# Layer 0 of an attention kernel: queries turned by VectorE in 32x32 blocks, output weights over 32 rows by head, four token quarters abreast

## The chip, the cores and the metric

The kernel runs on one core of one Trainium2 chip. A core has TensorE (PE in the profile; PEld is its weight loads), VectorE (DVE), ScalarE (ACT), GpSimd (POOL), and SyncE (SP), which here issues every DMA. The metric is the device time of one execution in microseconds; lower is better.

## The reference

Two layers, each a residual block over x of shape (16, 64, 64, 256) in f32. The change lies in layer 0, linear attention over the 4096 tokens of an image, with 8 heads of 32:

```
x = x + L0(gn(x))                       # gn: group norm, 32 groups
q, k, v = split(gn(x) @ w_qkv)          # 256 -> 3 * 256, each as 8 heads of 32
q = softmax(q over the 32 of a head) * 32**-0.5
k = softmax(k over the 4096 tokens)
context[h] = k[h] @ v[h].T              # 32 x 32 for a head
out = context[h].T @ q[h]; L0 = out @ w_out
x = x + L1(gn(x))                       # local attention, 7x7 windows, not changed
```

## The kernel before

Images run one after the other, 16 in all. An image is held as two tiles of 128 channels by 4096 tokens (`img`), `x` raw and `xn` normalised. Tokens are in 8 strips of 512; `strip(s)` is a strip's slice and `ORDER` the order in which layer 0 takes the strips. PE, ACT, DVE and SP run in the order in which the program is written (`manual_schedule`); an instruction that waits holds what is behind it on its engine. PSUM is used as two double banks, `double` (pd in the profile, handed out in turn by `psum2` and `bank`), and four single banks, `single` (ps).

Layer 0 of an image (`layer0`) goes through 16 pieces of 256 tokens:

- `queries_keys(p)`: PE multiplies tokens by the query and key weights (L514), ACT takes the exponential (L518), DVE sums the 32 of a head (L521) and takes the reciprocal (L523), POOL multiplies the query part by it (L524). The result `e` holds 128 tokens by 256 query and 256 key columns, twice.
- `context(p - 1)`: PE adds keys by tokens into `pc`, two banks of `single` (L532). The value weights come later, so the moving operand is the raw tokens `xtok`, loaded by DMA into one of two window buffers (`window`).
- `transposed(p - 2)`: four PE transposes (L546) of 128x128 turn the queries, so that the features of four heads lie on the 128 partitions; DVE (L552, even pieces) or ACT (L550, odd ones) copies them to `qq`.

Every second piece DVE also normalises the next strip (L283, through `normalise`).

After the 16 pieces, DVE scales and centres the context (L572, L573), and `output_weights` folds it with the value and output weights to `w2`, 256 by 256: transposes of the context (L301), a scaling (L306), products with the value weights (L311), the block diagonal of the heads (L319), products with `w_out` (L322), a scaling to `w2` (L323). For every strip PE then multiplies `qq` by `w2` (L587: for each half of the channels two matmuls of 128x128 by 512 columns that accumulate), DVE adds the result to x (L596) and takes the statistics for the next group norm (L473).

Then come the group norm of layer 1 (`group_steps`, L260 to L279), positional products (L630, evacuated to `qq` by DVE and ACT in turn, L621 and L619), values (L678), keys and queries (L704), and local attention for two groups of heads (L766 scores, L774 exponential, L784 and L797 weighted sums, `finish` with the block transposes L810 and L817). During local attention the next image is loaded and its first strips are normalised; the outputs of strips 1, 2 and 0 are stored last. `positional_products` takes its pairs of strips from `ORDER`; the values, keys and queries have an order of their own, `KEYED`.

Of the kernel before, what the change touches and what calls it, by code (L numbers as in the profile page):

```python
# [14 lines left out]
ALU = mybir.AluOpType  # L15
# [4 lines left out]
P = 128  # L20
W = 64
C = 256
HEADS, HD = 8, 32
NS = 8
# [9 lines left out]
SCALE = HD**-0.5  # L34
# [5 lines left out]

UNITS = (1, 2, 3, 0)
KEYED = (2, 3, 4, 5, 6, 7, 1, 0)
ORDER = (3, 4, 5, 6, 7, 1, 2, 0)
EDGE = (5, 3)


# [309 lines left out]
def attention_fast(tc, io, ok):  # L356


    nc = tc.nc
    with ExitStack() as ctx:  # L360
# [3 lines left out]
        double = [ps.tile([P, 2, 512], F32, tag=f"pd{i}", name=f"pd{i}") for i in range(2)]  # L364
        single = [ps.tile([P, 512], F32, tag=f"ps{i}", name=f"ps{i}") for i in range(4)]
        turn = [0, 0]

        def psum2():
            turn[0] += 1
            return double[turn[0] % 2]  # L370

        def banks():

            i = turn[1] % 4
            turn[1] += 1
            if i >= 2:
                return single[2 * i - 4 : 2 * i - 2], (0, 1)
            return [double[i][:, j] for j in range(2)], (i, i)
# [8 lines left out]
        n = Net(tc, cp, io)  # L387
# [3 lines left out]
        with tc.tile_pool(name="zeros", bufs=1) as zp:  # L391
# [3 lines left out]
            for v in vpad:  # L395
                rows = v.rearrange("a r w c -> a r (w c)")
# [7 lines left out]
            for d in pos:  # L404
                for i in range(2):
                    part = d[:, RING + 8 * i : RING + 8 * i + 8].rearrange("a s h w -> a (s h w)")
# [5 lines left out]
        qq = cp.tile([P, 2, NT], F32, tag="qq", name="qq")  # L412
# [7 lines left out]
        w2 = cp.tile([P, 2, C], F32, tag="w2", name="w2")  # L420
# [23 lines left out]
        def work_tile(name):  # L444
            return work.tile([P, 1024], F32, tag="work", name=name)

        def window(name):
            return vwin.tile([P, 2 * NB * P], F32, tag="vw", name=name)

        def watch(total, x, w):  # L450
            nc.gpsimd.tensor_tensor(total[:, :w], total[:, :w], x, ALU.add)  # L451

        def strip(s):
            return slice(s * 512, (s + 1) * 512)

        def halves(b):

            return [img[0][0], img[1][b % 2]], [img[0][1], img[1][1 - b % 2]]

        def load_half(b, k):  # L460
            x = halves(b)[0][k]
            for s in ORDER:
                nc.sync.dma_start(x[:, strip(s)], xc[b, :, k, strip(s)])
# [8 lines left out]
        def strip_stats(st, x, k, s):  # L472
            nc.vector.bn_stats(st[:, k, s], x[k][:, strip(s)])  # L473

        def stats_tile(name):
            return small.tile([P, 2, NS, 6], F32, tag="st", name=name)
# [23 lines left out]
        def layer0(b, x, xn, mean, rstd, xtok, ready):  # L500

            mu = None
            pc, other = single[:2], single[2:]
            eq = {}

            def first(p):
                return ORDER[p // 2] * 512 + (p % 2) * 2 * P

            def queries_keys(p):
                ps = psum2()  # L510
                for t in range(2):
                    n0 = first(p) + t * P
                    for k in range(2):
                        nc.tensor.matmul(  # L514
                            ps[:, t], xn[k][:, n0 : n0 + P], n.wqkv_sb[:, k, : 2 * C], start=(k == 0), stop=(k == 1)
                        )
                e = work_tile(f"eq{b}_{p}").rearrange("p (t c) -> p t c", t=2)
                nc.scalar.activation(e, ps, AF.Exp)  # L518
                q4 = e[:, :, :C].rearrange("p t (h d) -> p t h d", d=HD)
                z = small.tile([P, 2, HEADS], F32, tag="qz", name=f"qz{b}_{p}")  # L520
                nc.vector.tensor_reduce(z, q4, AX.X, ALU.add)  # L521
                r = small.tile([P, 2, HEADS], F32, tag="qr", name=f"qr{b}_{p}")
                nc.vector.reciprocal(r, z)  # L523
                nc.gpsimd.tensor_tensor(q4, q4, r.unsqueeze(3).to_broadcast([P, 2, HEADS, HD]), ALU.mult)  # L524
                watch(tops, r.rearrange("p t h -> p (t h)"), 2 * HEADS)
                watch(others, z.rearrange("p t h -> p (t h)"), 2 * HEADS)
                return e

            def context(p):
                for t in range(2):  # L530
                    for hg in range(2):
                        nc.tensor.matmul(  # L532
                            pc[hg][:, : C + 1],
                            eq[p][:, t, C + hg * P : C + (hg + 1) * P],
                            xtok[p // 4][:, 2 * (p % 4) + t],
                            start=(p == 0 and t == 0),
                            stop=(p == 15 and t == 1),
                        )

            def transposed(p):  # L540
                pt = other[p % 2]
                e = eq.pop(p)
                for hg in range(2):
                    for t in range(2):
                        i = 2 * hg + t
                        nc.tensor.transpose(pt[:, i * P : (i + 1) * P], e[:, t, hg * P : (hg + 1) * P], n.ident)  # L546
                dst = qq[:, :, first(p) : first(p) + 2 * P]
                src = pt.rearrange("p (g c) -> p g c", g=2)
                if p % 2:
                    nc.scalar.copy(dst, src)  # L550
                else:
                    nc.vector.tensor_copy(dst, src)  # L552

            for p in range(16 + 1):
                if p < 16:
                    if p % 2 == 0 and p // 2 + 1 < NS and p // 2 + 1 >= ready:
                        normalise(xn, x, mean, rstd, ORDER[p // 2 + 1])
                    eq[p] = queries_keys(p)
                if p == 1:
                    mu = n.spread(mean, lambda name: other[1], small, f"{b}")  # L560
                if 1 <= p <= 16:
                    context(p - 1)
                    if p % 4 == 0 and p // 4 + 1 < 4:
                        xtok[p // 4 + 1] = load_tokens(b, p // 4 + 1)
                if p >= 2:
                    transposed(p - 2)

            r = small.tile([P, 2, 1], F32, tag="krz", name=f"krz{b}")
            z = small.tile([P, 2, 1], F32, tag="kz", name=f"kz{b}")
            cc = work_tile(f"cc{b}")[:, : 2 * C].rearrange("p (a c) -> p a c", c=C)  # L570
            for hg in range(2):
                nc.vector.reciprocal(r[:, hg], pc[hg][:, C : C + 1])  # L572
                nc.vector.scalar_tensor_tensor(cc[:, hg], pc[hg][:, :C], r[:, hg], mu, ALU.mult, ALU.subtract)  # L573
            transposed(15)
            cT = work_tile(f"cT{b}")[:, :512].rearrange("p (a c) -> p a c", c=P)
            n.output_weights(cc, rstd, bank, cT, w2, f"{b}")
            for hg in range(2):
                nc.vector.tensor_copy(z[:, hg], pc[hg][:, C : C + 1])
            watch(tops, r.rearrange("p a b -> p (a b)"), 2)
            watch(others, z.rearrange("p a b -> p (a b)"), 2)  # L580

            st = stats_tile(f"st1_{b}")
            for s in ORDER:
                py, _ = banks()
                for hg in range(2):
                    for co in range(2):
                        nc.tensor.matmul(  # L587
                            py[co],
                            w2[:, hg, co * P : (co + 1) * P],
                            qq[:, hg, strip(s)],  # L590
                            start=(hg == 0),
                            stop=(hg == 1),
                        )
                for co in range(2):
                    xv = x[co][:, strip(s)]
                    nc.vector.tensor_tensor(xv, py[co], xv, ALU.add)  # L596
                for k in range(2):
                    strip_stats(st, x, k, s)
            return st

        def scale(to, w, rstd):
# [258 lines left out]
        with tc.manual_schedule(engines=ORDERED):  # L860
            x, xn = halves(0)
            st = stats_tile("st0_0")
            for k in range(2):
                load_half(0, k)
            for k in range(2):
                for s in ORDER:
                    strip_stats(st, x, k, s)
            gn = n.group_stats(st, 1e-5, small, bank, "0_0")
            xtok = {q: load_tokens(0, q) for q in range(2)}
            for s in ORDER[:2]:  # L870
                normalise(xn, x, *gn, s)
            for b in range(B):
                more = b + 1 < B
                x, xn = halves(b)
                st = layer0(b, x, xn, *gn, xtok, 2)
                mean, rstd = n.group_stats(st, 1e-5, small, bank, f"1_{b}")
                scale(wpos, n.wpos, rstd)
# [27 lines left out]
                if more:  # L905
                    st = stats_tile(f"st0_{b + 1}")
# [434 lines left out]
```

## Time and profile before

| | |
|---|---|
| time, median of 3 runs | 6052.62 us (6047.84 to 6058.84) |
| the profiled execution, its own time | 6068.61 us |
| its span in the trace | 6066.8 us |
| mean granted TensorE clock | 0.962 |
| PE busy | 5506.4 us (91%), 76913 matmul records |
| DVE, ACT, POOL busy | 2874.6 us (47%), 2254.7 us (37%), 1029.9 us (17%) |
| from one image's first L514 to the next's | 367.6 to 378.9 us |
| of that, to the start of L587 | 95.2 to 98.2 us |

Durations in the prediction are from the profiled execution, mostly from the second image (first L514 at 468.2 us), and its own time is 2 us longer than its span. A row of a group gives engine, operation, the tile that is written and those that are read, the shape (for PE the array's rows by columns used, then the shape of the moving operand), the count, then busy time and mean duration. An f32 matmul stands as two records, one for each pass, except a transpose, which is one. Durations of PE records have the latency in them; the distance between starts is what they cost in a stream. The chain that ended last is followed back from the last instruction; its list in order of time shows for each piece the start, the length, and the engine, tile and line, with the number of records.

### The profile page before, as it was taken

The page shows a single profiled execution, that of the slowest core. Times are in us where ns is not written, and L with a number is a line of the kernel's source. Part 1 is how long each engine was busy: PE and PEld are TensorE (multiplying, and loading weights), DVE is VectorE, ACT ScalarE, POOL GpSimd, SP SyncE. Part 2 cuts the span into 40 slices and gives each one's busy share as a digit, 9 for nine tenths or more (in the row PEclk, how much of TensorE's full clock was granted, in tenths as well). Part 3 has the DMA queues.
Part 4 walks back from the last instruction along what each step waited for, and adds up shares of the span by engine and source line. Part 5 has one row for each costly group of instructions (what it writes and reads, how often), then busy time and mean ns, then how long its engine had stood idle before and what let it go on. Part 6 is the DMA issues. An engine that isn't in the chain of part 4 may idle for free.

```text
span 6066.8 us, 171741 instructions
## 1 busy us (share of the span) xinstructions
PE 5506.4 (91%) x76913; PEld 3771.3 (62%) x76913; DVE 2874.6 (47%) x5034; ACT 2254.7 (37%) x3233; POOL 1029.9 (17%) x1945
## 2 busy tenths in 40 slices
PE   3999999898999989999898999999989999898998
PEld 2575665656656566665666657566565665756666
DVE  2544545445354444455444554454544545445354
ACT  0252433515334152342524425143252433415334
POOL 2012120211202113021120201212022120111202
PEclk9999999999999999999999999999999999999999
DMA  4341723516244252443515435163350724417234
GB/s 112 76 104 37 133 80 79 115 45 129 59 96 104 48 121 59 102 104 66 110 44 114 99 74 103 37 129 84 73 112 31 144 66 83 104 39 141 59 76 82
DMA packets 737035, 526.94 MB, mean 87 GB/s; under 512 B 240400, under 2 KB 667664, under 8 KB 733712
## 3 DMA queue, kind: packets, MB, share of 16 engines
q1 hardware_dynamic: 736288, 515.86, 38.9%
q8 instruction: 605, 9.91, 0.7%
q14 instruction: 142, 1.16, 0.1%
HBM read 357.02 MB, written 158.73 MB: 85 GB/s over the span
## 4 chain that ended last, share of the span: by engine, by line
PE 88%; ACT 4%; issue 4%; DVE 2%; SPq 1%; DMA 0%; POOL 0%; ACTq 0%; DVEq 0%; POOLq 0%
PE pd L766 16%; PE ps L797 16%; PE pd L514 15%; PE pd L704 7%; PE ps L532 7%; PE ps L704 5%; ACT qq L619 4%; PE pd L587 4%; PE ps L678 4%; PE pd L678 4%; PE ps L587 4%; PE ps L630 2%; PE ps L546 2%; PE ps L784 1%; SPq L399 1%
## 5 line engine op out<-in xcount | busy, mean ns | idle before, releaser
L774 ACT ACTIVATE e<-pd 128x896 f32<-128x896 f32 (+2 forms) x1152 | 928.5, 839 | 1132.0 <-PE pd L766 1129.4
L766 PE MATMUL pd<-qq,kaug 64*64 64x140 f32 (+5 forms) x27648 | 1052.3, 294 | 218.4 <-ACT e L774 143.5
L766 PEld LDWEIGHTS pd<-qq,kaug 64*64 64x64 f32 x27648 | 923.8, 140 | 354.4 <-issue 163.6
L514 PE MATMUL pd<-wqkv,img 128*128 128x512 f32 x2048 | 923.3, 595 | 1.7 <-DVE img L283 1.6
L797 PE MATMUL ps<-e,vw 128*32 128x112 f32 (+1 forms) x18432 | 853.8, 260 | 63.4 <-issue 63.0
L797 PE MATMUL ps<-e,ones 128*32 128x112 f32 (+1 forms) x18432 | 846.5, 256 | 59.7 <-issue 59.2
L810 DVE STREAM_TRANSPOSE r<-ps 128x512 f32<-128x512 f32 x256 | 168.8, 696 | 1437.6 <-PE ps L797 1437.3
L451 POOL TENSOR_TENSOR others<-others,rc 128x16 f32<-128x16 f32 x256 | 113.1, 442 | 2981.5 <-DVE rc L815 2981.5
L518 ACT ACTIVATE eq<-pd 128x1024 f32<-128x1024 f32 x256 | 261.9, 1023 | 943.3 <-PE pd L514 943.3
L514 PEld LDWEIGHTS pd<-wqkv,img 128*128 128x128 f32 x2048 | 372.6, 191 | 380.6 <-issue 353.3
L797 PEld LDWEIGHTS ps<-e,vw 128*32 128x32 f32 x18432 | 502.9, 113 | 154.9 <-issue 117.7
L797 PEld LDWEIGHTS ps<-e,ones 128*32 128x32 f32 x18432 | 546.5, 114 | 72.4 <-issue 71.8
L619 ACT ACTIVATE qq<-ps,bias 32x512 f32<-32x512 f32 (+2 forms) x544 | 320.2, 622 | 718.1 <-PE ps L630 712.5
L521 DVE TENSOR_REDUCE qz<-eq 128x16 f32<-128x512 f32 x256 | 175.5, 685 | 830.5 <-ACT eq L518 830.5
L532 PE MATMUL ps<-xtok,eq 128*128 128x257 f32 x2048 | 486.1, 380 | 0.0
L532 PEld LDWEIGHTS ps<-xtok,eq 128*128 128x128 f32 x2048 | 386.1, 190 | 149.0 <-issue 107.1
L830 POOL TENSOR_TENSOR img<-img,r 128x320 f32<-128x320 f32 (+1 forms) x512 | 421.5, 844 | 164.8 <-DVE rc L815 163.5
L619 ACT ACTIVATE kaug<-pd,bias 32x512 f32<-32x512 f32 x256 | 173.7, 679 | 633.6 <-PE pd L704 630.7
L473 DVE BATCH_NORM_STATS2 st<-img 128x6 f32<-128x512 f32 x512 | 319.9, 677 | 66.1 <-DMA img<-in_xc 66.1
L621 DVE TENSOR_SCALAR qq<-ps,bias 32x512 f32<-32x512 f32 x384 | 309.3, 806 | 6.8
L524 POOL TENSOR_TENSOR eq<-eq,qr 128x512 f32<-128x512 f32 x256 | 274.7, 1073 | 30.7 <-DVE qr L523 1.2
L821 DVE TENSOR_TENSOR r<-r 128x512 f32<-128x512 f32 x256 | 222.3, 868 | 27.5 <-DVE r L817 0.5
(126 smaller groups left out, 6170.0 us busy)
## 6 DMA issues: line engine op xcount, KB each, us to landing
vw<-vpad SPq DMA_DIRECT2D x512, 288.0 KB
img<-in_xc SPq DMA_DIRECT2D x256, 256.0 KB
xtok<-in_xt SPq DMA_DIRECT2D x64, 1024.0 KB
out<-img SPq DMA_DIRECT2D x256, 256.0 KB
vpad<-v SPq DMA_DIRECT2D x112, 512.0 KB
qq<-pos SPq DMA_DIRECT2D x128, 256.0 KB
qq<-in_ring SPq DMA_DIRECT2D x128, 256.0 KB
pos<-qq SPq DMA_DIRECT2D x128, 112.0 KB
```

What stands on the lines that cost most here:

```text
L473: nc.vector.bn_stats(st[:, k, s], x[k][:, strip(s)])
L514: nc.tensor.matmul(ps[:, t], xn[k][:, n0 : n0 + P], n.wqkv_sb[:, k, : 2 * C], start=(k == 0), stop=(k == 1))
L532: nc.tensor.matmul(pc[hg][:, : C + 1], eq[p][:, t, C + hg * P : C + (hg + 1) * P], xtok[p // 4][:, 2 * (p % 4) + t], start=(p == 0 and t = ...
L587: nc.tensor.matmul(py[co], w2[:, hg, co * P : (co + 1) * P], qq[:, hg, strip(s)], start=(hg == 0), stop=(hg == 1),)
L619: nc.scalar.activation(dst, src, AF.Identity, bias=bias)
L621: nc.vector.tensor_scalar(dst, src, bias, None, ALU.add)
L678: nc.tensor.matmul(pi[:, t], x[k][:, n0 : n0 + P], wv[:, k], start=(k == 0), stop=(k == 1))
L704: nc.tensor.matmul(ps[a], wgt[:, k, hg * P : (hg + 1) * P], x[k][:, strip(pair[a])], start=(k == 0), stop=(k == 1),)
L766: nc.tensor.matmul(to, kaug[pl][rows, u, 8 * c : 8 * c + 8].rearrange("p r w -> p (r w)"), q, start=True, stop=True,)
L774: nc.scalar.activation(e, ps[:, :, : 2 * m], AF.Exp)
L797: nc.tensor.matmul(dst, ones if to is zs[j] else vw[:, j, c, h * HD : (h + 1) * HD], pr, start=False, stop=(c == NB - 1),)
L830: nc.gpsimd.tensor_tensor(yv, xv, by_rows(add[:, :, a - w0 : e - w0], xv), ALU.add)
```

## The change

The queries are turned by DVE instead of PE. A DVE transpose of 128x256 turns each 32x32 block by itself, so a quarter of 32 tokens stays on its 32 partitions, which then hold the 32 features of a head; the heads lie one after the other in the free dimension. `qq` is seen as `qv`: partitions (quarter, feature), then 8 heads by 1024 tokens. The output weights are thus needed per head over 32 rows, once in each of the four row groups: `w4`, which takes one of the window buffers. It is made by products of 32 columns whose moving operand repeats a head's context four times, and products over 32 rows. The output product then runs one matmul of 32 rows by 128 columns by 256 tokens for each head, quarter and channel half; the four quarters go to four banks. Results are added per quarter, with a stride in x. `ORDER` is now made of pairs of neighbouring strips, since the product takes 1024 tokens at a time; the host packs the tokens in the same order.

```diff
--- before.py
+++ after.py
@@ -40,7 +40,7 @@
 
 UNITS = (1, 2, 3, 0)
 KEYED = (2, 3, 4, 5, 6, 7, 1, 0)
-ORDER = (3, 4, 5, 6, 7, 1, 2, 0)
+ORDER = (4, 5, 6, 7, 0, 1, 2, 3)
 EDGE = (5, 3)
 
 
@@ -503,6 +503,8 @@
             pc, other = single[:2], single[2:]
             eq = {}
 
+            qv = qq.rearrange("p g (h n) -> p (g h) n", h=4)
             def first(p):
                 return ORDER[p // 2] * 512 + (p % 2) * 2 * P
 
@@ -537,19 +539,12 @@
                             stop=(p == 15 and t == 1),
                         )
 
-            def transposed(p):
-                pt = other[p % 2]
+            def turned(p):
                 e = eq.pop(p)
-                for hg in range(2):
-                    for t in range(2):
-                        i = 2 * hg + t
-                        nc.tensor.transpose(pt[:, i * P : (i + 1) * P], e[:, t, hg * P : (hg + 1) * P], n.ident)
-                dst = qq[:, :, first(p) : first(p) + 2 * P]
-                src = pt.rearrange("p (g c) -> p g c", g=2)
-                if p % 2:
-                    nc.scalar.copy(dst, src)
-                else:
-                    nc.vector.tensor_copy(dst, src)
+                for t in range(2):
+                    T = 2 * p + t
+                    nc.vector.transpose(qv[:, :, HD * T : HD * T + HD], e[:, t, :C].rearrange("p (h d) -> p h d", d=HD))
 
             for p in range(16 + 1):
                 if p < 16:
@@ -563,7 +558,7 @@
                     if p % 4 == 0 and p // 4 + 1 < 4:
                         xtok[p // 4 + 1] = load_tokens(b, p // 4 + 1)
                 if p >= 2:
-                    transposed(p - 2)
+                    turned(p - 2)
 
             r = small.tile([P, 2, 1], F32, tag="krz", name=f"krz{b}")
             z = small.tile([P, 2, 1], F32, tag="kz", name=f"kz{b}")
@@ -571,31 +566,77 @@
             for hg in range(2):
                 nc.vector.reciprocal(r[:, hg], pc[hg][:, C : C + 1])
                 nc.vector.scalar_tensor_tensor(cc[:, hg], pc[hg][:, :C], r[:, hg], mu, ALU.mult, ALU.subtract)
-            transposed(15)
-            cT = work_tile(f"cT{b}")[:, :512].rearrange("p (a c) -> p a c", c=P)
-            n.output_weights(cc, rstd, bank, cT, w2, f"{b}")
+            turned(15)
+            ct = work_tile(f"ct{b}")
+            cT, ch = ct[:, :512].rearrange("p (a c) -> p a c", c=P), ct[:, 512:768]
+            for hg in range(2):
+                for k in range(2):
+                    nc.tensor.transpose(
+                        other[0][:, (2 * k + hg) * P : (2 * k + hg + 1) * P], cc[:, hg, k * P : (k + 1) * P], n.ident
+                    )
+            for k in range(2):
+                dst = cT[:, 2 * k : 2 * k + 2].rearrange("p a b -> p (a b)")
+                nc.vector.tensor_scalar(dst, other[0][:, k * C : (k + 1) * C], rstd[:, k : k + 1], None, ALU.mult)
+            for hg in range(2):
+                for k in range(2):
+                    for h in range(4):
+                        rows = slice(HD * h, HD * h + HD)
+                        nc.tensor.matmul(
+                            other[1][rows, hg * P : (hg + 1) * P].rearrange("p (a d) -> p a d", a=4),
+                            n.wqkv_sb[:, k, 2 * C + hg * P + HD * h : 2 * C + hg * P + HD * h + HD],
+                            cT[:, 2 * k + hg, rows].unsqueeze(1).to_broadcast([P, 4, HD]),
+                            start=(k == 0),
+                            stop=(k == 1),
+                        )
+            nc.vector.tensor_scalar(ch, other[1][:, :C], SCALE, None, ALU.mult)
+            for hg in range(2):
+                for h in range(4):
+                    rows = slice(HD * h, HD * h + HD)
+                    nc.tensor.matmul(
+                        double[h // 2][:, h % 2, hg * C : (hg + 1) * C],
+                        ch[rows, hg * P : (hg + 1) * P],
+                        n.wout_sb[rows, hg],
+                        start=True,
+                        stop=True,
+                    )
             for hg in range(2):
                 nc.vector.tensor_copy(z[:, hg], pc[hg][:, C : C + 1])
+            w4 = window(f"w4_{b}")[:, : 8 * C].rearrange("p (h g c) -> p h g c", h=4, g=2)
+            for h in range(2):
+                nc.vector.tensor_copy(w4[:, h].rearrange("p g c -> p (g c)"), double[0][:, h])
+            nc.scalar.copy(w4[:, 2:4].rearrange("p h g c -> p h (g c)"), double[1])
             watch(tops, r.rearrange("p a b -> p (a b)"), 2)
             watch(others, z.rearrange("p a b -> p (a b)"), 2)
 
             st = stats_tile(f"st1_{b}")
-            for s in ORDER:
-                py, _ = banks()
-                for hg in range(2):
-                    for co in range(2):
-                        nc.tensor.matmul(
-                            py[co],
-                            w2[:, hg, co * P : (co + 1) * P],
-                            qq[:, hg, strip(s)],
-                            start=(hg == 0),
-                            stop=(hg == 1),
-                        )
+            for i in range(NS // 2):
+                s0 = ORDER[2 * i]
                 for co in range(2):
-                    xv = x[co][:, strip(s)]
-                    nc.vector.tensor_tensor(xv, py[co], xv, ALU.add)
-                for k in range(2):
-                    strip_stats(st, x, k, s)
+                    py = [double[a // 2][:, a % 2, : 2 * P] if co else single[a][:, : 2 * P] for a in range(4)]
+                    for h in range(4):
+                        for hg in range(2):
+                            for a in range(4):
+                                rows = slice(HD * a, HD * a + HD)
+                                nc.tensor.matmul(
+                                    py[a],
+                                    w4[rows, h, hg, co * P : (co + 1) * P],
+                                    qv[rows, 4 * hg + h, 8 * HD * i : 8 * HD * (i + 1)],
+                                    start=(h == 0 and hg == 0),
+                                    stop=(h == 3 and hg == 1),
+                                )
+                    xv = x[co][:, s0 * 512 : (s0 + 2) * 512].rearrange("p (t a n) -> p a t n", a=4, n=HD)
+                    if co:
+                        for a in (0, 2):
+                            part = double[a // 2][:, :, : 2 * P].rearrange("p a (t n) -> p a t n", n=HD)
+                            nc.vector.tensor_tensor(xv[:, a : a + 2], part, xv[:, a : a + 2], ALU.add)
+                    else:
+                        for a in range(4):
+                            nc.vector.tensor_tensor(xv[:, a], py[a].rearrange("p (t n) -> p t n", n=HD), xv[:, a], ALU.add)
+                    for s in (s0, s0 + 1):
+                        strip_stats(st, x, co, s)
             return st
 
         def scale(to, w, rstd):
```

## The prediction

> **What bounds the kernel now.** I read the page first: engine totals, then the chain that ended last.
>
> ```profile
> PE 5506.4 (91%) x76913; PEld 3771.3 (62%) x76913; DVE 2874.6 (47%) x5034; ACT 2254.7 (37%) x3233; POOL 1029.9 (17%) x1945
> ...
> PE 88%; ACT 4%; issue 4%; DVE 2%; SPq 1%; DMA 0%; POOL 0%; ACTq 0%; DVEq 0%; POOLq 0%
> ...
> PE pd L766 16%; PE ps L797 16%; PE pd L514 15%; PE pd L704 7%; PE ps L532 7%; PE ps L704 5%; ACT qq L619 4%; PE pd L587 4%; PE ps L678 4%; PE pd L678 4%; PE ps L587 4%; PE ps L630 2%; PE ps L546 2%; PE ps L784 1%; SPq L399 1%
> ```
>
> TensorE is busy 91% and holds 88% of the chain, so what leaves TensorE's stream shortens the time. The change touches L546 (query transposes, 2%) and L587 (output product, 4% + 4%). The chain in order of time, over layer 0 of the second image, shows the stage (start, length, work):
>
> ```profile
> 544.49 3.44 PE pd L514 x8
> 547.92 1.74 PE ps L532 x8
> 549.66 0.44 PE ps L546 x4
> 550.09 3.44 PE pd L514 x8
> ...
> 557.44 0.45 PE ps L546 x4
> 557.89 0.03 issue
> 557.91 0.69 DVE qq L552
> 558.61 0.08 DVE krz L572
> ...
> 563.34 7.13 PE pd L587 x16
> ...
> 584.21 6.88 PE ps L587 x16
> 591.09 0.02 issue
> 591.12 0.69 DVE img L596
> 591.81 1.19 DVE st L473 x2
> ```
>
> A piece of 256 tokens is 3.44 + 1.74 + 0.44 = 5.6 us of TensorE without a gap; nothing else is in the chain there. From the end of L514 (553.53) to the start of L587 (563.34) come 9.8 us of short dependent steps, the "turn". L587 is again TensorE alone; 6.87 us for 16 records of 512 columns is 0.429 us each, 0.839 ns per column and pass (an f32 matmul is two records). After L587 statistics follow, and TensorE waits until 596.88.
>
> **What tells how four row groups behave.** No f32 product of the kernel before uses 32 rows; three things come near. The timeline of TensorE shows L784, which has the very tile shape (32 rows by 128 columns, four row groups, four banks), in bf16:
>
> ```profile
> 320.42 0.39 PE L784 MATMUL ps<-zb 32*128 32x512 bf16 x4
> 320.74 0.32 PE L797 MATMUL ps<-e,vw 128*32 128x64 f32 x8
> ```
>
> The next work starts 0.32 us after the first of the four. One after another at the f32 pass's 0.429 us they would need 1.7 us, and at half of that 0.86. The chain gives the f32 tiles of layer 1:
>
> ```profile
> 679.90 1.68 PE pd L766 x37
> 681.58 1.67 PE ps L797 x64
> ```
>
> Each row covers two window steps. A step of L766 has 12 matmuls in 64x64 tiles (two row halves, two column halves), of 14 x 10, 14 x 16 and 14 x 6 columns: 3584 column passes, which alone would take 3.0 us; two steps in 1.68 us means 3.6 abreast, of four. L797 (four column groups of 32, 16 matmuls of 112 columns a step) gives 3.6 too.
>
> **The Trainium skill.** "TensorEngine Tiling (Array Packing)", Tiling Modes and Gotcha 1: row tiles of 32 rows run independently if they write different banks. The change gives each quarter its own bank; L784 agrees. "TensorE: Matmul & The Clock Gate", Part 3, Measured speedup: four row tiles of K=32, N=512 gave 3.07x; the 3.6 above is better, since it is a stream. Same page, LDWEIGHTS: a load costs its columns, whatever the rows. The trace agrees in order: 190 ns for 128 columns (L587), 140 for 64 (L766), 113 for 32 (L797). Same page, Part 1: idle of about 3.4 us halves the clock. The trace agrees: granted clock 0.75 in 591 to 597 and 0.79 in 597 to 606.
>
> **The change, part by part, per image.**
>
> Transposes of the pieces. The 64 of L546 go. Thirteen groups of four stand ahead of the last L514: 13 x 0.44 = **5.7 us off**. The other three lie in the turn. With them go 8 VectorE copies of 0.69 us (L552) and 8 ScalarE copies of 0.59 (L550), both hidden. Added are 32 VectorE block transposes of 128x256. L810 takes 0.696 us for 128x512, and an operation from PSUM costs 0.69 at 512 elements (L596) and 0.424 at 256 (L323), so 256 elements are worth 0.27: estimate 0.44 us each, 0.35 apart when queued. VectorE per piece: reduction 0.69, reciprocal 0.25, transposes 0.8, half of two normalisations 0.87, together 2.6 of 5.2 us, hidden behind TensorE. Queued behind them are the next normalisation and reduction; ScalarE and POOL then have the same slack as before. Bounds: 0.35 to 0.9 us each (the destination is eight runs 4 KB apart); even 0.9 leaves the piece hidden (3.6 of 5.2), but the turn grows.
>
> The turn. L514 ends at 553.53, the two last L532 groups at 557.0. VectorE is free of the reciprocal at 555.79, then has four transposes, until 557.3. The reciprocal of the key sums starts there, not at 558.52; the two centred contexts take 1.27 as now: 558.6. The last two transposes stand ahead of the scaling of the turned context: 559.4 (now 560.32). From there to the last product of L311 takes 1.87 now; sixteen 32-column matmuls, four abreast, stream the same 8 x 0.107: 561.3. One scaling of 128x256, 0.42: 561.7. Eight 32-row products, two rounds of two passes of 0.215, and about 0.27 of load and latency: 562.8. The first copy of weights, 0.69: the output product starts at about 563.6 against 563.34: **0.3 us on** (bounds: 0.5 off to 2 on). VectorE's second copy is there by 564.2, wanted at 564.5; ScalarE copies the other half in 1.02 us (L518's 1024 elements), wanted at 565.3.
>
> Output product. 32 matmuls of 512 columns become 256 of 256: 128 rounds of four passes, 128 x 256 x 0.839 ns = 27.5 us, the same as 64 x 0.429. L797's round costs 0.104 against 0.094 of streaming; 128 such margins are 1.3 us. Bounds 0 to 1.3; I take half, **0.7 us on**, since longer streams hide more. VectorE's evacuation per 1024 tokens: four adds of 0.42, two of 0.69, four statistics of 0.68, together 5.8 of 6.9 us: hidden.
>
> End of it. Both column halves used to end one after the other; now all four banks of the last half end together, and two adds and two statistics follow: 0.6 + 0.69 + 1.19 = 2.5 us against 1.9: **0.6 us on**.
>
> Clock. The turn has more idle on TensorE and the wait after it is longer. In 8 of the 16 images the trace has the half clock in the turn, and the output product starts 96 us after the first L514 instead of 95.2; I allow that in the other half too: **0.5 us on** (bounds 0 to 2).
>
> Order of strips. Loads, stores, tokens and normalisation follow it. What comes earlier is strip 0: normalised ahead of piece 8, not 14. Its buffer's store is the last of attention, issued on SP's queue by 476.6, and the DMA share is 0 from 480; the normalisation comes after the fifth piece's reduction, near 498. Hidden by 18 us; without that cover VectorE would hold the next reduction. In the ring positions strip 0's edge pieces move from ScalarE to VectorE, about 0.5 us, behind TensorE's L630 and L889. The copied weights take one of two window buffers; the load that reuses it is queued after all value stores, past 635. No new wait on SP or POOL.
>
> Sum: -5.7 + 0.3 + 0.7 + 0.6 + 0.5 = -3.6 us an image, -58 us for 16. The profiled execution took 6068.6 us (span 6066.8): 6011. The median of three is 16 us (0.26%) below it: **5995 us**.
>
> **Rivals.**
> 1. Weight loads stick out (ends slower). 256 columns of streaming hide less than 512. If each round waited for its load, 128 x 0.107 us (L546 shows one 128-column load and one 128-column pass per 0.109 us) = 13.7 us an image: 16 x 10.1 = +162, 6215 us. It decides from 28 ns exposed per round, where 3.6 us is used up. For it: loads of 128 columns are twice L766's. Against: L766 runs a load and a pass every 35 ns, so loads of different tiles overlap each other and the streaming.
> 2. Row groups share something in f32. Two abreast: +27.5 - 3.6 an image, 6434 us; none: +82.5 - 3.6, 7257 us. Against: L784 and L766, whose two row halves write the same partitions.
> 3. The gain is eaten in the gaps: transposes at 0.9 us add 1.8 to the turn, or the slow clock comes each time (2 us): 6020 to 6055 us. For it: the turn already hangs on VectorE. That the change does not do what it says would be this: VectorE's turning would show up in the chain in place of L546.
>
> **How the numbers follow.** Forecast 0.68, within 5950 to 6030; rival 3 0.15; rival 1 0.10; rival 2 0.07. About 0.2% (12 us) is what a measurement can tell from no change. Faster: 0.68 and most of rival 3, 0.78; same 0.04; slower 0.18. The range, 5950 to 6060, leaves out rivals 1 and 2.
>
> **What would show it.** Right: pieces 5.17 us apart in the chain, no L546; the output product 27.5 to 29 us of TensorE an image, with some 0.22 us per round; block transposes of 128x256 at 0.4 to 0.5 us outside the chain. Wrong: an output product above 31 us (rivals 1, 2), or VectorE entries between L514 groups (rival 3).

## The result and the profile after

The changed kernel takes 6006.96 us (median of 5 runs, 6002.63 to 6025.9) against 6052.62: a ratio of 0.9927 with a 95% interval of 0.9909 to 0.9946. It is faster by 0.7%; the forecast was 5995. Its profiled execution took 6006.96 us, with a span of 6005.2 us against 6066.8.

The page of the changed kernel, engine totals:

```profile
PE 5397.6 (90%) x83633; PEld 3876.1 (65%) x83633; DVE 2954.2 (49%) x5562; ACT 2196.0 (37%) x3089; POOL 1025.1 (17%) x1945
```

TensorE has 6720 more matmul records and 109 us less of busy time; VectorE has 80 us more. The chain on this page follows only 2% of the span back, so it can't stand beside the chain of before. I use timelines of one engine, and for each image the distances between the first records of the same lines. Four groups of the changed kernel follow: L547 stands in place of L546, L550 and L552, L637 (with L634) in place of L596, L623 in place of L587 (other lines moved: L514 is L516, L630 is L671, L678 is L719):

```profile
L547 DVE STREAM_TRANSPOSE qq<-eq 128x256 f32<-128x256 f32 x512 | 181.1, 394 | 0.3 <-issue 0.2
L637 DVE TENSOR_TENSOR img<-ps,img 128x256 f32<-128x256 f32 x256 | 90.7, 417 | 103.6 <-PE ps L623 103.6
L623 PE MATMUL ps<-qq,w 32*128 32x256 f32 x4096 | 246.4, 390 | 12.4 <-DVE w L608 12.4
L623 PE MATMUL pd<-qq,w 32*128 32x256 f32 x4096 | 232.2, 374 | 0.0
```

The block transposes cost 0.394 us each, and VectorE sat idle ahead of them for only 0.3 us in the whole execution: what they read was there when VectorE came to them. The two L623 groups hold TensorE for 246 + 232 = 479 us; before, the two L587 groups held it for 229 + 225 = 454.

From the third on, the pieces stand 5.17 us apart, as forecast. This is TensorE's timeline of the changed kernel at the end of layer 0 of the fifth image:

```profile
1689.98 3.63 PE L623 MATMUL ps<-qq,w 32*128 32x256 f32 x64
1693.44 3.63 PE L623 MATMUL pd<-qq,w 32*128 32x256 f32 x64
1700.47 0.59 PE L266 MATMUL pd<-gn,grp 128*128 128x2 f32 x2 [3.40 <-DVE gn L263]
1701.89 0.59 PE L275 MATMUL pd<-gnd,grp 128*128 128x2 f32 x2 [0.84 <-DVE gnd L272]
1703.81 3.68 PE L671 MATMUL ps<-img,wposn 128*64 128x512 f32 x8 [1.32 <-DVE wposn L644]
1707.27 0.59 PE L653 MATMUL pd<-gnm,wposn 128*64 128x1 f32 x8
1707.66 6.39 PE L671 MATMUL ps<-img,wposn 128*64 128x512 f32 x24
1713.99 1.13 PE L930 MATMUL pd<-wvn,gnm 128*128 128x256 f32 x4
1716.78 0.48 PE L719 MATMUL pd<-wvn,img 128*128 128x256 f32 x1 [1.66 <-DVE bvn L933]
```

A half product is 64 records of 256 columns, and the next starts 3.46 us later: 16 rounds of four at 0.216 us, against 0.215 of pure streaming (256 x 0.839 ns). The four quarters run fully abreast, and the loads of weights are hidden. The last row was not foreseen: the first value product waits 1.66 us for VectorE's bias sum (L933). In the sixth image the same place has no wait:

```profile
2080.26 1.13 PE L930 MATMUL pd<-wvn,gnm 128*128 128x256 f32 x4
2081.22 7.07 PE L719 MATMUL pd<-wvn,img 128*128 128x256 f32 x32
```

From the answer on that line of the changed kernel, TensorE's matmuls alone:

```profile
L719 PE MATMUL pd<-wvn,img x1024: 379/379/483, 235.7 to 5783.7; 128*128 128x256 f32 x171
...
  DVE bvn L933: 14.7, 8
```

The second of these rows stands under the times that the engine sat idle ahead of the line: 14.7 us in 8 times, 1.8 us each. They fall in every second image, the first, third, fifth and so on. For the kernel before (L678) no idle time stands there.

Where each image's time stands, in us between starts of records, mean of the 16 images. The sum is the distance from image to image, mean of the 15 full ones, and the row above it is what is left of that sum:

| step | before | after | forecast of the difference | measured |
|---|---|---|---|---|
| first to last L514 record (pieces) | 85.03 | 79.29 | -5.7 | -5.74 |
| to the first output product (turn) | 10.83 | 10.62 | +0.3 | -0.21 |
| to the last output record | 27.28 | 28.32 | +0.7, clock +0.5 | +1.04 |
| to the aggregation L260 | 2.43 | 2.94 | +0.6 | +0.51 |
| to the first positional product | 3.97 | 3.94 | 0 | -0.03 |
| to the first value product | 10.26 | 11.71 | 0 | **+1.45** |
| to the next image | 232.29 | 231.89 | 0 | -0.40 |
| sum | 372.09 | 368.71 | -3.6 | -3.38 |

The step to the first value product takes 12.92 us in the images with the wait and 10.49 in the others. The step to the next image varies by some 10 us from image to image in both kernels (228 to 238 us), so its -0.40 can't be told from nothing.

### The profile page after: what moved, and what is told of

The parts are those of the page before. It is cut to its first block, busy times and chain, and to the rows that moved or that the text cites. A ratio compares the mean times of both kernels' runs of the same rounds, so it can differ in the third digit from the quotient of the medians.

```text
span 6005.2 us, 185440 instructions
## 1 busy us (share of the span) xinstructions
PE 5397.6 (90%) x83633; PEld 3876.1 (65%) x83633; DVE 2954.2 (49%) x5562; ACT 2196.0 (37%) x3089; POOL 1025.1 (17%) x1945
## 5 line engine op out<-in xcount | busy, mean ns | idle before, releaser
L807 PE MATMUL pd<-qq,kaug 64*64 64x224 f32 (+5 forms) x27648 | 1043.4, 293 | 237.3 <-ACT e L815 144.8
L516 PE MATMUL pd<-wqkv,img 128*128 128x512 f32 x2048 | 922.4, 594 | 1.6 <-DVE img L283 1.6
L516 PEld LDWEIGHTS pd<-wqkv,img 128*128 128x128 f32 x2048 | 388.6, 190 | 392.2 <-issue 358.4
L520 ACT ACTIVATE eq<-pd 128x1024 f32<-128x1024 f32 x256 | 262.2, 1024 | 1013.3 <-PE pd L516 1010.6
L662 DVE TENSOR_SCALAR qq<-ps,bias 32x512 f32<-32x512 f32 (+2 forms) x416 | 313.1, 761 | 7.0
L623 PE MATMUL ps<-qq,w 32*128 32x256 f32 x4096 | 246.4, 390 | 12.4 <-DVE w L608 12.4
```

The source lines that it names most:

```text
L516: nc.tensor.matmul(ps[:, t], xn[k][:, n0 : n0 + P], n.wqkv_sb[:, k, : 2 * C], start=(k == 0), stop=(k == 1))
L623: nc.tensor.matmul(py[a], w4[rows, h, hg, co * P : (co + 1) * P], qv[rows, 4 * hg + h, 8 * HD * i : 8 * HD * (i + 1)], start=(h == 0 and h ...
L662: nc.vector.tensor_scalar(dst, src, bias, None, ALU.add)
L807: nc.tensor.matmul(to, kaug[pl][rows, u, 8 * c : 8 * c + 8].rearrange("p r w -> p (r w)"), q, start=True, stop=True,)
```

## The experiments

Each run's ratio is to the kernel before, run beside it on the same chip: 6053.73 us for the first four, 6062.35 for the next four, 6059.93 for the last.

**The wait at the values.** `psum2` and `bank` hand out the two double banks in turn. The old layer 0 took 21 of them (16 pieces, 5 in `output_weights`), the new one takes 16. The rest of an image takes 77 (2 in the statistics, 3 with the biases, 72 in the scores), so that an image took 98 turns, an even number, and now takes 93, an odd one. The value products start in double bank 0 always (`banks` has a counter of its own). The bias product L930 used to fall into the other bank in every image; now its bank alternates, and in every second image it falls into that same bank. One more turn makes the count even again:

```diff
                         strip_stats(st, x, co, s)
+            psum2()
             return st
```

> The changed kernel with one more turn of the double banks at the end of layer 0, so that the bias product for the values (L930 in the changed kernel) again falls into the other bank than the first value products (L719). Theory A (the miss against the forecast is a bank collision: the change asks for 16 double banks in layer 0 instead of 21, so the first value product waits for VectorE's bias sum behind 7.8 us of positional evacuations): the step from the first positional product to the first value product falls from 11.7 us (mean of the 16 images) to some 10.2, 1.5 us an image, 24 us in all, about 5983 us (ratio to the kernel before 0.988 to 0.989). Rival B (that wait is taken up later, or the step is long because the half clock falls there): the step or what follows stays long and the time is within 6 us of 6007.

Measured: 5990.04 us, 0.9875 (0.985 to 0.9899). The step to the first value product is 10.63 us, and no image has the wait. VectorE's queue is as long as before, but TensorE no longer waits for it; these are TensorE's and VectorE's timelines of e1_other_bank around the same place:

```profile
1701.79 1.13 PE L931 MATMUL pd<-wvn,gnm 128*128 128x256 f32 x4
1702.75 5.56 PE L720 MATMUL pd<-wvn,img 128*128 128x256 f32 x25
```

```profile
1696.90 7.66 DVE L663 TENSOR_SCALAR qq<-ps,bias 32x512 f32<-32x512 f32 x10
1704.59 0.42 DVE L934 TENSOR_TENSOR bvn<-bv,pd 128x256 f32<-128x256 f32 x1
```

The values start at 1702.75, ahead of the bias sum at 1704.59. Theory A stands as to the collision, though it put the wait in every image: of the 24 us that it asked for, 17 came back by the medians and by the steps, 31 by the ratios to the kernel before, whose intervals are wide. The step ends where the changed kernel's images without the wait stand (10.49), not at the 10.26 of before; what else lies in it is the half clock, further below.

The same line put into the kernel before, at the end of its `layer0`:

> The kernel before with the same one turn of the double banks at the end of layer 0, nothing else. Theory A: the same collision arises without the change: VectorE ends its evacuations and the bias sum at 1719.3 us in the fifth image where TensorE wants the bank at 1716.9, so up to 2.4 us an image, 24 to 38 us slower than before (6077 to 6090 us). Rival B: the collision needs strip 0 among VectorE's evacuations or the changed pairs: within 0.2% of before.

Measured: 6076.71 us, 1.0035 (1.0023 to 1.0047). The step goes from 10.26 to 11.22 us in the mean: 12.53 in every second image and 9.90 in the others. The wait appears in the kernel before, where the line is L679 (TensorE's matmuls alone):

```profile
L679 PE MATMUL pd<-wvn,img x1024: 379/379/634, 240.2 to 5859.2; 128*128 128x256 f32 x171
...
  DVE bvn L893: 18.0, 8
```

18.0 us of waiting in 8 images go with 21 us of time (23 by the medians). That is just under theory A's span of 24 to 38 us, which had the wait in all 16 images; 8 times its 2.4 us would be 19. The collision needs nothing of the change but an odd count of turns.

**The transposes.** Put back on TensorE for pieces 0 to 12, read by nobody:

```diff
                 e = eq.pop(p)
+                for i in range(4 if p < 13 else 0):
+                    nc.tensor.transpose(
+                        other[p % 2][:, i * P : (i + 1) * P], e[:, i % 2, (i // 2) * P : (i // 2 + 1) * P], n.ident
+                    )
                 for t in range(2):
```

> The changed kernel with the TensorE transposes of pieces 0 to 12 put back, their results read by nobody; VectorE still turns the queries. Theory A (the gain is the 13 x 0.44 us that left TensorE's stream ahead of the last L514): 5.7 us an image, 91 us, about 6098 us, pieces 5.6 us apart. Rival B (the gain came from the copies taken off ScalarE and VectorE, or the pieces are bound elsewhere): within 20 us of 6007.

Measured: 6093.59 us, 1.0055 (1.0033 to 1.0077). That is 87 us above the changed kernel by the medians and 77 by the ratios, where 91 were expected. The last L516 stands again at 84.97 us after the first. The gain in the pieces is what left TensorE's stream: VectorE turned the queries here too, with ScalarE and VectorE free of the copies.

**The order of strips**, alone in the kernel before:

```diff
-ORDER = (3, 4, 5, 6, 7, 1, 2, 0)
+ORDER = (4, 5, 6, 7, 0, 1, 2, 3)
```

> The kernel before with the new order of strips alone (4 5 6 7 0 1 2 3). Theory A (the order is hidden, 18 us between the store of strip 0 and its normalisation): within 0.2% of before. Rival B (strip 0's pieces on VectorE or its late store cost something): 0.5 us or more an image, 8 us or more slower, seen between positional products and values or as a wait of the normalisation.

Measured: 6058.91 us, 1.0004 (0.9991 to 1.0016). No step moves by more than 0.2 us. The order is hidden, as theory A has it.

**The four quarters abreast.**

```diff
-                    for h in range(4):
-                        for hg in range(2):
-                            for a in range(4):
+                    for a in range(4):
+                        for h in range(4):
+                            for hg in range(2):
```

> The changed kernel with the output product's loop over the four quarters outermost: eight matmuls of one row group in a row, then the next quarter's. Same instructions, same count. Theory A (four row groups stream at the same time, and only if they stand next to each other in the stream): the groups come one after another, 256 matmuls x 2 passes x 0.216 us = 110 us an image instead of 27.5, 82 us an image, about 7320 us. Rival B (the engine reorders across row groups by itself, or the product is bound by something else than the streams): far less, within 300 us of 6007.

Measured: one run of 8262.28 us. The output product lasts 168.7 us an image. Theory A holds as to the cause, and its size is off twice. The windows of the first image's product tell why (columns: length, then busy time and count of each engine, then the granted clock):

```profile
190.00:350.00 160.00, 160.00 (x485) 131.33 (x484) 20.63 (x37) 0.00 (x0) 0.00 (x0) 0.50 0.00 0
```

TensorE is never idle by its records, yet the clock is at one half throughout. In the first 2 us, at full clock, a pass starts every 0.216 us; then every 0.427 within a quarter. 512 x 0.427 would be 219 us; at the seams between quarters passes of both overlap, and 169 are left. At full clock that would be some 84 us, an estimate by halving, against 27.5 abreast.

**The half clock in the turn.** In 7 images of the changed kernel the half clock comes within the turn, and in 6 of them it reaches into the output product. Fillers (matmuls whose result nobody reads) in e1_other_bank, ahead of the context's transposes, of the value products and of the 32-row products, and after these:

```diff
+            def filler(bank, k):
+                for _ in range(k):
+                    nc.tensor.matmul(bank, zb, zb[:, :1].to_broadcast([P, 512]), start=True, stop=True)
             ct = work_tile(f"ct{b}")
+            filler(double[1][:, 0], 4)
...
+            filler(double[1][:, 0], 2)
...
+            filler(other[0], 2)
...
+            filler(other[0], 3)
```

> e1_other_bank with 11 bf16 matmuls of 512 columns in the idle gaps of the turn (4 ahead of the context's transposes, 2 ahead of the value products, 2 ahead of and 3 after the 32-row products), into banks that nobody reads. Theory A (the half clock in the turn costs the difference between disturbed and undisturbed images, last output product at 117.98 us in the mean against 116.77): no half clock in the turn, 1.2 us an image, 19 us below e1_other_bank (5990): about 5971. Rival B (zeros do not count as activity for the clock, or the fillers delay the short steps by as much): within 6 us of e1_other_bank, with the half clock still in the turn or the product's start later than 89.23.

Measured: 5969.92 us, 0.9849 (0.9827 to 0.9871). The second image's turn and the first 8 us of its output product, first e1_other_bank, then e6_warm_turn (the granted clock is the third figure from the end):

```profile
546.00:558.00 12.00, 9.24 (x75) 5.94 (x73) 6.18 (x19) 1.84 (x2) 1.84 (x5) 0.81 0.01 1
558.00:566.00 8.00, 8.00 (x96) 6.82 (x100) 1.90 (x6) 0.19 (x1) 0.00 (x0) 0.64 0.01 2
```

```profile
541.00:551.00 10.00, 9.44 (x79) 5.68 (x79) 6.04 (x19) 1.70 (x2) 1.84 (x5) 1.00 0.01 3
551.00:559.00 8.00, 7.99 (x148) 7.60 (x152) 4.03 (x9) 0.33 (x1) 0.00 (x0) 1.00 0.01 2
```

0.81 and 0.64 become 1.00, in every image, and the last output record stands at 116.91 us after the first L516 in the mean, not 117.98. The two ratios' intervals just overlap; the trace's 1.1 us an image are 17 us. Theory A holds by the trace.

**VectorE's queue in the turn.**

```diff
-                if p >= 2:
+                if 2 <= p < 16:
                     turned(p - 2)
...
-            turned(15)
...
                 nc.vector.tensor_scalar(dst, other[0][:, k * C : (k + 1) * C], rstd[:, k : k + 1], None, ALU.mult)
+            turned(14)
...
             watch(others, z.rearrange("p a b -> p (a b)"), 2)
+            turned(15)
```

> e1_other_bank with VectorE's transposes of piece 14 moved behind the scaling of the turned context, and those of piece 15 behind the copies of the weights, so that neither stands ahead of the context's steps. Theory A (VectorE's queue is what the turn hangs on): the output product starts 0.4 to 0.5 us earlier (88.8 instead of 89.23 after the first L516), 7 us in all. Rival B (the chain of the turn is TensorE's and the waits' alone): start unchanged at 89.2, no difference.

Measured: 5987.69 us, 0.9879 (0.9859 to 0.99): by the times not told apart from e1_other_bank. By the trace the output product starts 88.87 us after the first L516 in every image but the first (theory A: 88.8), and VectorE now waits for the last context product, where in the changed kernel it came late to it. VectorE's timelines, first of the changed kernel (the four transposes, then straight on), then of e7_late_turn:

```profile
1661.81 1.36 DVE L547 STREAM_TRANSPOSE qq<-eq 128x256 f32<-128x256 f32 x4
1663.09 0.13 DVE L567 RECIPROCAL krz<-ps 128x1 f32<-128x1 f32 x1
```

```profile
1651.80 0.71 DVE L547 STREAM_TRANSPOSE qq<-eq 128x256 f32<-128x256 f32 x2
1652.70 0.17 DVE L567 RECIPROCAL krz<-ps 128x1 f32<-128x1 f32 x1 [0.20 <-PE ps L534]
```

The mean of the last output record is 116.51 (117.98 in e1_other_bank). Of this some 1.1 us is no work of the queue: in no image of that profile does the half clock come within the turn, though nothing was put there to prevent it. The images stand 366.74 us apart (367.84 in e1_other_bank), and this does not show in the medians. The profiled execution of e7_late_turn was the fastest of its five and that of e1_other_bank the second slowest of its six; why the medians lie only 2 us apart stays open.

**All of it, and the same for the statistics gap.**

```diff
-                mean, rstd = n.group_stats(st, 1e-5, small, bank, f"1_{b}")
+                got = []
+                parts = n.group_steps(st, 1e-5, small, bank, f"1_{b}", got)
+                for k in (10, 4, 6):
+                    next(parts, None)
+                    filler(single[3], k)
+                mean, rstd = got
```

> e6_warm_turn and e7_late_turn together, and 20 more such fillers in the statistics gap after the output product (10, 4 and 6 ahead of the three steps on TensorE). Theory A (the half clock of 6.8 us falls on the positional products in every image and costs some 1.5 us there): the step from the first positional to the first value product falls from 10.6 to about 9.1 us; with the other two, some 50 us below e1_other_bank, about 5940 us. Rival B (the fillers delay the statistics, or the clock falls all the same): 5960 us or more, with the positional products starting later than 3.98 us after the aggregation.

Measured: 5921.98 us, 0.9769 (0.9749 to 0.9789). The step to the first value product falls to 8.27 us in every image, further than the 9.1 expected, and the positional products start 3.77 us after the aggregation. This version beats both kernels, by 2.3% and some 1.6%.

How much of that belongs to the change? The statistics fillers alone in the kernel before, into `double[0][:, 1]`:

> The kernel before with the 20 fillers in the statistics gap alone (10, 4 and 6 ahead of the three steps on TensorE, into the half of a double bank that nobody reads). Theory A (the half clock on the positional products is as old as the kernel and independent of the change): the step from the first positional to the first value product, 10.26 us in the mean, falls to about 9.0, some 20 us (0.33%) faster than before, about 6033 us. Rival B (it is the change's longer gap that makes the fillers pay): within 0.1% of before.

Measured: 6027.92 us, 0.9945 (0.9927 to 0.9963); the step falls from 10.26 to 8.27 us, 2.0 us an image. The granted clock over the second image's positional products goes from 0.79 in the kernel before to 1.00 here:

```profile
597.00:606.00 9.00, 9.00 (x40) 3.23 (x40) 4.96 (x8) 3.12 (x4) 0.00 (x0) 0.79 0.00 0
```

```profile
600.00:609.00 9.00, 9.00 (x48) 4.08 (x47) 6.53 (x11) 4.30 (x5) 0.26 (x1) 1.00 0.01 2
```

So the half clock there is no work of the change. Of e8_warm_both's 2.3%, 0.55% is to be had without the change.

## Why the prediction was right, point by point

**Pieces.** -5.7 forecast, -5.74 measured, and e3_pe_turns takes it back. VectorE's transposes were estimated at 0.44 us and took 0.394, hidden but for those in the turn.

**Turn.** +0.3 forecast; in the images without the half clock it went from 10.41 to 10.11 us, so -0.3. VectorE's queue was reckoned too dear: the four transposes took 1.36 us, not 1.49, the steps on the context were shorter too, and the scaling L581 began 5.89 us after the last L516, not 6.46. That the turn hangs on VectorE's queue was right: e7_late_turn takes another 0.36 us off.

**Output product.** +0.7 forecast for margins between rounds. At full clock it went from 27.57 to 27.76 us (27.14 and 27.54 between first and last start, with the last pass of 0.429 and 0.215). The margin per round is 1 ns and not L797's 10. A load of 128 columns over 32 rows took 185 to 209 ns in the mean in the second image, as over 128 rows before (190), and the rounds hide it. Rivals 1 and 2 fall with the 0.216 us a round; e5_one_quarter shows what one group at a time costs. Rival 2's last figure is a slip: none abreast, +82.5 - 3.6 us an image on top of 6053, would be 7315 us, not 7257.

**Clock.** +0.5 forecast. In images without the half clock the turn and product together changed by +0.1 us, in the mean by +0.83; so the clock took 0.7 us more than before. The size is near, but the reason given for it, the half clock in the other half of the images too, did not come: it fell in the turn of 7 images, against 8 before. It cost more because in 6 of them it lasted into the output product, for 1.5 to 2.7 us each; before, that was 0.5 to 0.7 us in 4 images. That the size came out is luck.

**End.** +0.6 forecast, +0.51 between starts, +0.7 with the shorter last pass.

**The step that failed** is the list of what waits: "No new wait on SP or POOL" is true but looked at the wrong queues. The psum banks were followed only within layer 0. The removed `output_weights` took five turns of a shared counter with it, and TensorE got a new wait far behind the change, in every second image. The step there grew by 1.45 us in the mean, 23 us in all; some 19 of these are the wait's (12.92 against 10.49 us in 8 images). e1_other_bank takes back 17 us by the medians, and e2_before_bank makes the wait in the kernel before. Rival 3 had the size of such a loss, not its place.

**The sum.** -3.6 an image forecast, -3.38 in the profile: the errors, -0.5 in the turn, -0.2 in product and clock together, -0.1 at the end, +1.45 at the values and -0.40 after them, nearly cancel. That the sum came closer than its parts is luck. The 12 us between forecast and median also hold the way from profile to median: the profiled execution of before lay 16 us above its median, the one of after is its median.

## What to carry to other kernels

Count what a removed helper took from shared rotations. Where the turns of one pass through the loop go from even to odd, a later product's bank alternates, and in every second pass two users can meet in one bank far behind the change; one dummy turn mended it here. A mean over the images hides such a thing, so look at the images one by one. When small products are packed into row groups, put the loop over the groups innermost: here only neighbours in the stream ran abreast. The short chain of the statistics cost twice in both kernels, once as idle and once as half clock after it; matmuls into an unread bank covered it cheaply.

## What the runs showed of the hardware

- Four f32 row groups of 32 by 128 with four banks stream without loss: 0.216 us for four passes of 256 columns, with a 128-column weight load behind each.
- One row group at a time, with TensorE busy all the time, brought the clock to 0.50 within 2 us, and it stayed there for the 160 us read above. The full array kept 1.00 (the pieces), and so did four groups, in the images where the half clock had not come within the turn. Whether rows in use or the rate of products decides was not tried.
- Matmuls of zeros in bf16, put into the gaps, kept the clock at full speed: 1.00 in place of 0.64 after the turn, and 1.00 in place of 0.79 after the statistics gap, worth 2.0 us an image there.
